# A four-layer modulated convolution on one core: a shorter first chain, a third pair of output banks, and row ends blurred on VectorE

## The chip, the cores and the metric

The kernel runs on one core of a Trainium2 chip. The metric is the device time of one execution in microseconds. Each execution is one launch over all 128 samples. TensorE (PE in the profile, its weight loads PEld) does the matrix products, VectorE (DVE) and ScalarE (ACT) read its results from PSUM and do the vector work, GpSimd (POOL) does small vector work in SBUF, and SyncE (SP) issues nearly all transfers.

## The reference, cut to what matters

Every sample has its own weights: a style vector of 128 numbers is mapped to one scale per input channel and layer, and the scaled weights are normalised for every output channel. Four convolution layers of 64 channels follow, and the input is added to their result.

```python
def _layer(x, style, w, b, mw, mb, typ):
    s = style @ mw.T + mb
    weight = SCALE * w * s[:, None, :, None]
    demod = lax.rsqrt(jnp.sum(weight * weight, axis=(2, 3)) + EPS)
    weight = weight * demod[:, :, None, None]
    if typ == 'same':
        out = vmap(_conv_same)(x, weight) + b
    elif typ == 'upsample':                 # stride 2, then blur
        out = _blur(vmap(_conv_up)(x, weight) + b, 2.0 * blur_k, (1, 1))
    elif typ == 'downsample':               # blur, then stride 2
        out = vmap(_conv_down)(_blur(x, blur_k, (2, 2)), weight) + b
    return out
...
for i, typ in enumerate(('same', 'upsample', 'same', 'downsample')):
    out = _layer(out, style, weights[i], biases[i], mod_w[i], mod_b[i], typ)
return x + out          # x: 128 x 64 x 1024, float32
```

The blur kernel is (1, 3, 3, 1)/8. No nonlinearity stands between the layers, so all four collapse, for each sample, into one convolution with nine taps. Only the first and last three columns of a row differ, because of the padding.

## The kernel before

**The work.** Two samples make a pair `p` (64 pairs), four samples, or two pairs, a step `q` (32 steps, `p = 2q` and `2q + 1`). For each `q` the combined weights are made by a chain of matrix products: `scale3` scales the last layer's weights (`wd`), `stage1` multiplies them with layer 2 (`psS`, copied to `S`), `stage2` with the blurred layer 1 (`psR`, copied to `R`), `stage3` in two parts with layer 0 (`psW`, copied to `Wf`). `combine` makes sums `H` of them for a fast convolution. On the data side `pre1` and `pre2` make sums `T` (and `G` on the way) of the input planes `X`: two operations on VectorE for `G`, two for `T` (lines 478 and 479, by default on GpSimd), and `pre2a` and `pre2b` on VectorE. `convA12` and `convA3` multiply three of these sums with `H` into a PSUM tile `psA`. `seed1` combines these into `u`, `v` and `y1`, and `seed2` writes two sums into the output banks `Y`. `convB` adds two further products to what lies in `Y`. `output` scales, adds the constant and moves the result to `o`, and `store` sends it off. So VectorE must have written `Y` (`seed2`) before TensorE may start `convB` of that pair, and it may write `Y` only after the outputs of the pair before have been read.

**The banks.** PSUM has two buffers of two banks for `ps_conv` (in turn `psM`, some `psS`, `psR`, all `psA`), two banks for `ps_w` and two for `Y`. From the last steps on, `Y2` turns the pair of `ps_w` into a second pair of output banks, for pairs 60 and 62; pairs 61 and 63 stay on `Y`. `zeros_to_y` runs products of zeros over a pair of output banks before its first use. Two early calls of it (lines 845 and 851) stand where TensorE would otherwise have nothing to do.

**The order.** The order of each engine's instructions is that of the program; it is written out by hand. Lines 839 to 919 are the prologue. The first 16 samples (`PART[0]`) come first: `mod_matmul` and `mod_scale` give the layers' scales, `var_matmul` (line 204), `var_root` and the Newton steps give the norms. Layer 2's norm is inverted first (`first_inverse`), since `table_A` and with it `scale3(0)` need it; those of the other layers follow (`var_inverse`, `var_newton`, lines 866 and 867). `blur_matmul` (line 288) needs the transfer `par_oi`. Two later groups of samples (`PART[1]`, `PART[2]`) get their scales and norms later; `mod_matmul(LATER)` in line 871 makes the scales of both.

**The main loop**, lines 993 to 1077, has the same order for each `q`: `stage2(q+2)`, `convB(p)`, its outputs, `stage3(q+2, 0)`, `convA12(p+2)`, VectorE work for later pairs, `stage3(q+2, 1)`, `convA3(p+2)`, `convB(p+1)`, its outputs, VectorE work, `stage1(q+3)`, `scale3(q+4)`, `combine(q+2)`, `convA12` and `convA3` of `p+3`. The first steps and the last two differ a little.

**The row ends.** The first and last three columns of all rows are computed apart and layer by layer, in `SLOTS` (small groups of matmuls between the two products of a `convB`) and `EXTRA` (VectorE work at the two halves of a step). For the last layer `setup2` blurs its weights into six taps `g3`, and `ends3` runs those six taps over `Ve`, the end columns of layer 2's output.

## Time and profile before

| | |
|---|---|
| time, median of 3 runs | 503.1 us (502.73 to 504.3) |
| time of the profiled execution | 505.0 us |
| its span, first to last instruction | 503.2 us |
| mean granted TensorE clock | 0.995 |
| TensorE busy | 490.7 us, 98% of the span |
| VectorE busy | 438.9 us, 87% |
| ScalarE busy | 322.3 us, 64% |
| GpSimd busy | 127.7 us, 25% |
| DMA | 70.90 MB, mean 141 GB/s |

A record in the profile has a start, a duration and the engine's idle time before it, with what ended that idle time. Matmuls are pipelined [...], so the duration of one (304 ns) says less than the distance between two starts; every matmul of the program leaves two records. In the timeline, neighbouring records of one kind are merged: a row gives the first start, the time to the last end and how many there are.

### The profile page before, as it was taken

The page shows a single profiled execution, that of the slowest core. Times are in us where ns is not written, and L with a number is a line of the kernel's source. Part 1 is how long each engine was busy: PE and PEld are TensorE (multiplying, and loading weights), DVE is VectorE, ACT ScalarE, POOL GpSimd, SP SyncE. Part 2 cuts the span into 40 slices and gives each one's busy share as a digit, 9 for nine tenths or more (in the row PEclk, how much of TensorE's full clock was granted, in tenths as well). Part 3 has the DMA queues.
Part 4 walks back from the last instruction along what each step waited for, and adds up shares of the span by engine and source line. Part 5 has one row for each costly group of instructions (what it writes and reads, how often), then busy time and mean ns, then how long its engine had stood idle before and what let it go on. Part 6 is the DMA issues. An engine that isn't in the chain of part 4 may idle for free.

```text
span 503.2 us, 28357 instructions
## 1 busy us (share of the span) xinstructions
PE 490.7 (98%) x12644; PEld 479.4 (95%) x12644; DVE 438.9 (87%) x932; ACT 322.3 (64%) x785; POOL 127.7 (25%) x192
## 2 busy tenths in 40 slices
PE   8999899999999999999999999999999999999994
PEld 5889799999999999999999999999999999999994
DVE  4789989999999979988979999879988879888895
ACT  3446466676676666676677666657667657667653
POOL 3414122334222122122222122212212212222210
PEclk9999999999999999999999999999999999999999
DMA  8115544444444444443544444435454435443123
GB/s 258 59 45 171 179 128 131 160 145 142 142 157 149 151 142 138 148 147 122 157 144 148 132 154 153 146 128 162 125 164 146 139 120 185 138 151 129 66 107 126
DMA packets 37161, 70.90 MB, mean 141 GB/s; under 512 B 4144, under 2 KB 28464, under 8 KB 37040
## 3 DMA queue, kind: packets, MB, share of 16 engines
q1 hardware_dynamic: 36960, 68.85, 42.3%
q8 instruction: 99, 1.62, 1.4%
q10 hardware_dynamic: 80, 0.25, 0.1%
q14 instruction: 22, 0.18, 0.1%
HBM read 35.46 MB, written 33.62 MB: 137 GB/s over the span
## 4 chain that ended last, share of the span: by engine, by line
PE 85%; DVE 10%; ACT 2%; issue 1%; DMA 1%; DVEq 0%
PE psA L516 28%; PE Y L516 20%; PE psR L365 15%; PE psW L402 13%; PE psS L334 6%; PE psE L747 2%; DVE Y L549 2%; DVE T L498 1%; PE Y L170 1%; DVE G L469 1%; ACT o L595 1%; DVE T L488 1%; PE psM L189 1%; DVE v L549 1%; DVE G L472 1%
## 5 line engine op out<-in xcount | busy, mean ns | idle before, releaser
L516 PE MATMUL psA<-T,H 64*64 64x170 f32 x4608 | 207.7, 304 | 0.9 <-DVE H L443 0.9
L516 PEld LDWEIGHTS psA<-T,H 64*64 64x64 f32 x4608 | 191.2, 133 | 1.5 <-ACT R L312 1.2
L516 PE MATMUL Y<-T,Wf 64*64 64x170 f32 x3072 | 143.2, 307 | 4.3 <-DVE Y L549 4.3
L478 POOL TENSOR_TENSOR T<-G 128x342 f32<-128x342 f32 x60 | 55.1, 919 | 338.2 <-DVE G L472 193.5
L516 PEld LDWEIGHTS Y<-T,Wf 64*64 64x64 f32 x3072 | 130.5, 134 | 5.7 <-issue 3.9
L595 ACT ACTIVATE o<-Y,oc,dm 128x340 f32<-128x340 f32 (+1 forms) x126 | 80.0, 635 | 58.8 <-PE Y L516 56.5
L549 DVE SCALAR_TENSOR_TENSOR Y<-psA,u 128x340 f32<-128x340 f32 (+1 forms) x132 | 66.4, 507 | 42.4 <-ACT o L595 40.2
L402 PE MATMUL psW<-R,par_oi 64*64 64x256 f32 (+3 forms) x1536 | 100.4, 349 | 0.0
L365 PE MATMUL psR<-S,E 64*64 64x192 f32 (+1 forms) x2304 | 94.0, 299 | 0.0
L312 ACT ACTIVATE Wf<-psW,t 128x256 f32<-128x256 f32 (+1 forms) x252 | 75.5, 382 | 22.9 <-PE psW L402 22.9
L402 PEld LDWEIGHTS psW<-R,par_oi 64*64 64x64 f32 x1536 | 87.0, 133 | 2.3
L365 PEld LDWEIGHTS psR<-S,E 64*64 64x64 f32 x2304 | 86.5, 133 | 0.8 <-ACT Wf L312 0.3
L312 ACT ACTIVATE R<-psR,tC 128x448 f32<-128x448 f32 x63 | 36.6, 631 | 56.7 <-PE psR L365 56.7
L595 ACT ACTIVATE o<-y,oc,dm 128x170 f32<-128x170 f32 x125 | 65.7, 526 | 0.0
L498 DVE TENSOR_TENSOR T<-G 128x684 f32<-128x684 f32 x64 | 56.1, 877 | 0.0
L469 DVE SCALAR_TENSOR_TENSOR G<-X 128x688 f32<-128x688 f32 x64 | 55.4, 866 | 0.0
L479 POOL TENSOR_TENSOR T<-G 128x342 f32<-128x342 f32 x60 | 55.3, 922 | 0.0
L334 PE MATMUL psS<-wd,par_oi 64*64 64x192 f32 x768 | 46.2, 332 | 0.1
L334 PEld LDWEIGHTS psS<-wd,par_oi 64*64 64x64 f32 x768 | 38.0, 137 | 1.3 <-ACT wd L312 0.3
L543 ACT ACTIVATE m<-psA 128x340 f32<-128x340 f32 x64 | 29.3, 457 | 11.6 <-PE psA L516 6.5
L549 DVE SCALAR_TENSOR_TENSOR y<-psA,v 128x340 f32<-128x340 f32 x64 | 32.7, 511 | 2.2
L549 DVE SCALAR_TENSOR_TENSOR u<-psA,m 128x340 f32<-128x340 f32 x64 | 32.2, 503 | 0.5 <-ACT m L543 0.5
(127 smaller groups left out, 386.2 us busy)
## 6 DMA issues: line engine op xcount, KB each, us to landing
out<-o SPq DMA_DIRECT2D x128, 255.0 KB, 2.8
X<-in_x SPq DMA_DIRECT2D x60, 344.0 KB, 3.1
X<-in_x SPq DMA_DIRECT2D x60, 172.0 KB, 3.0
X<-in_x SPq DMA_DIRECT2D x4, 516.0 KB, 6.9
Xe<-in_x_ends SPq DMA_DIRECT2D x1, 512.0 KB, 3.7
par_oi<-in_params_oi SPq DMA_DIRECT2D x2, 208.0 KB, 4.8
par_io<-in_params_io ACTq DMA_DIRECT2D x1, 240.0 KB, 3.8
par_io<-in_params_io SPq DMA_DIRECT2D x1, 240.0 KB, 4.4
```

The lines of the kernel that those rows point to most:

```text
L312: nc_a.activation(dst, src, AF.Copy, scale=f)
L334: nc.tensor.matmul(ps[r][cols, k * C : (k + K) * C], woi[rows, 2, k, :], src[rows, :], start=(k == 0), stop=(k == K - 1), skip_group_check ...
L365: nc.tensor.matmul(ps[r][cols, lo * C : (lo + m) * C], E[rows, e // 2 + 1 + (e % 2) * 5, :], src[rows, a, :], start=(n == 0), stop=(n == 8 ...
L402: nc.tensor.matmul(ps[r][cols, (lo - t_lo) * C : (hi - t_lo) * C], woi[rows, 0, k, :], rt[c][rows, lo - k : hi - k, :], start=(k == order[0]),
L469: nc_v.scalar_tensor_tensor(g[:, PL:], X[:, : 2 * PL], 0.5, X[:, PL:], op0=ALU.mult, op1=ALU.subtract)
L478: eng.tensor_add(t[:, 2, :NJ], plane(g, 2), plane(g, 1))
L479: eng.tensor_sub(t[:, 3, :NJ], plane(g, 2), plane(g, 1))
L498: nc_v.tensor_sub(t[:, 0:2, :NJ], both(a, PL), both(b, 1))
L516: nc.tensor.matmul(ps[s][cols], w, Ts[p][rows, SLOT[m], j : j + NB], start=(g == 0 and m not in (0, 4)), stop=(g == 2), skip_group_check=True,
L543: nc_a.activation(m1, m[0], AF.Copy, scale=-1.0)
L549: nc_v.scalar_tensor_tensor(out, x, f, y, op0=ALU.mult, op1=ALU.add)
L595: nc_a.activation(dst, src, AF.Identity, bias=add, scale=d3)
```

## The change

**Prologue.** Layer 2 goes alone through square, sum, `var_matmul`, `var_root` and `first_inverse`. The squares of layers 0 and 1 (VectorE) and 3 (ScalarE), their sums and their `var_matmul` come later, the latter between the matmuls of `stage1(0)` and the copies of its result. Half of the second group of zero products is left out. `mod_matmul(LATER)` moves from before `stage2(0)` to after `stage2(1)`, into a buffer of its own (`psL`), and what hangs on it (`mod_scale(PART[1])`, tables) moves too. The constant products of layers 1 and 2 for `PART[0]` and `var_matmul(PART[1])` come later, the last into free columns of an output bank. The sums of the first input pairs are reordered: `pre1(0)` is split into its two operations for `G` and the two for `T`, with copies of the weight chain between them. The norms of `PART[1]` (`var_inverse`, `var_newton`, `table_A`, tables) move from the prologue into the first step. In that step `pre1(4)` and `pre1(5)` lose the argument `nc_v`, so that lines 478 and 479 run on GpSimd for them, `seed1(3)` comes ahead of `pre1(5)`, and in step 1 `seed2(3)` comes ahead of `pre1(6)`.

**Last pair.** Pair 63 gets a third pair of output banks, taken from `ps_conv`, with its own `zeros_to_y`; its whole `seed` then runs in step 30. Its stores are split into columns of the first third and of the other two thirds.

**Row ends.** `g3` and `setup2` go. `blur_side` adds neighbouring columns of `Ve` three times (six operations on VectorE, steps 20 to 23), which is the blur (1, 3, 3, 1) without its factor; `ends3` then has three taps with the plain weights, and `rest3` multiplies by 0.125.

```diff
-        nc_v.tensor_mul(ssq[:, :, bs], sc[:, :, bs], sc[:, :, bs])
...
+    def mod_square(bs, ls=slice(0, NL)):
+        nc_v.tensor_mul(ssq[:, ls, bs], sc[:, ls, bs], sc[:, ls, bs])
+
+    def q2_sum(ls):
+        nc_v.tensor_add(q2[T, ls], wsq[T, ls, 0, :], wsq[T, ls, 1, :])
+        nc_v.tensor_add(q2[T, ls], q2[T, ls], wsq[T, ls, 2, :])
...
-            return rest
+            return g01, g2, rest
...
-    def store(p, s):
-        nc.sync.dma_start(out[p, :, s], os[p][:, s])
+    def store(p, s, at=slice(0, 3 * NB)):
+        nc.sync.dma_start(out[p, :, s, at], os[p][:, s, at])
...
+    def blur_side(s, part):
+        at = (2 * s, 0, 0)[part]
+        src = (Ve[s], Ue[s], Ve[s])[part][:, :, at : at + 10 - part]
+        dst = (Ue[s], Ve[s], Ue[s])[part][:, :, : 9 - part]
+        nc_v.tensor_tensor(dst, src[:, :, :-1], src[:, :, 1:], op=ALU.add)
+
     def ends3(ps):
...
-            6,
-            lambda i, r, c: g3[:, i, :],
-            lambda i, r, c: Ve[c][:, :, i + 2 * c : i + 2 * c + 5 : 2],
+            K,
+            lambda i, r, c: wio[:, 3, i, :],
+            lambda i, r, c: Ue[c][:, :, i : i + 5 : 2],
...
-    nc_a.activation(wsq[T, :2], wio[T, :2], AF.Square)
-    nc_v.tensor_mul(wsq[T, 2:], wio[T, 2:], wio[T, 2:])
+    nc_a.activation(wsq[T, L2], wio[T, L2], AF.Square)
     blur_scale()
-    zeros_to_y(4, 256)
+    zeros_to_y(2, 256)
     mod_scale(PART[0], pm[0][0])
-    nc_v.tensor_add(q2[T], wsq[T, :, 0, :], wsq[T, :, 1, :])
-    nc_v.tensor_add(q2[T], q2[T], wsq[T, :, 2, :])
-    for table_of in (table_B, table_0, table_02):
-        table_of(PART[0])
-    var_matmul(PART[0], pm[0][1])
-    var_root(PART[0], pm[0][1])
+    mod_square(PART[0])
+    q2_sum(L2)
+    table_B(PART[0])
+    weight_sums()
+    var_matmul(PART[0], pm[0][1], (2,))
+    nc_v.tensor_mul(wsq[T, L01], wio[T, L01], wio[T, L01])
+    var_root(PART[0], pm[0][1], L2)
+    nc_a.activation(wsq[T, L3], wio[T, L3], AF.Square)
     psB = [Y[:, r] for r in range(2)]
     blur_matmul(psB)
-    weight_sums()
     first_inverse(PART[0])
     table_A(PART[0], d2)
     scale3(0, BOTH)
+    q2_sum(L01)
     blur_copy(psB, BOTH)
+    q2_sum(L3)
+    table_0(PART[0])
+    table_02(PART[0])
+
+    def rest_of_var():
+        var_matmul(PART[0], pm[0][1], (0, 1, 3))
+
+    stage1(0, None, BOTH, rest_of_var)
+    var_root(PART[0], pm[0][1])
+    scale3(1)
+    scale3(2)
     var_inverse(PART[0])
     var_newton(PART[0])
...
-    stage1(0, None, BOTH)
-    mod_matmul(LATER, pm[1][0])
-    scale3(1)
-    nc_a.copy(raw[0][:, 0, :n_later], pm[1][0][:, :n_later])
-    scale3(2)
-    pre1(0, nc_v)
...
+    g01, g2, t12 = pre1(0, None)
+    g01()
+    stage2(0, None, BOTH)
+    zeros_to_y(2, 512)
+    const_first(0, PART[0])
+    g2()
+    t12(nc_v)
+    pre2a(0)
+    stage3(0, 0, None, BOTH)
+    stage1(1, ps_conv)
+    pre2b(0)
+    g01, g2, t12 = pre1(1, None)
+    g01()
+    stage3(0, 1, None, BOTH)
+    stage1(2, ps_conv)
+    combine(0)
+    const_rest(0, PART[0], const_of(0, PART[0]))
+    stage2(1, ps_conv)
+    psL = unit(ps_conv, "psL")
+    mod_matmul(LATER, psL[0])
+    nc_a.copy(raw[0][:, 0, :n_later], psL[0][:, :n_later])
+    convA12(0)
+    convA3(0)
...
     stage3(1, 1)
+    const_first(2, PART[0])
+    var_matmul(PART[1], var_of(PART[1]), start=False)
     convA3(1)
+    pre1(2)
+    pre2(2)
+    const_rest(2, PART[0], const_of(2, PART[0]))
+    var_root(PART[1], var_of(PART[1]))
     combine(1)
-    pre2a(2)
+    seed1(1)
     pre1(3)
-    seed1(1)
-    pre2b(2)
-    var_inverse(PART[1])
-    var_newton(PART[1])
-    table_A(PART[1], dm[:, 2, PART[1]])
-    for of in (table_C, vector_c0, table_3, vector_Da):
-        of(PART[1])
...
-        (17, 0): lambda: setup2(0),
-        (17, 1): lambda: setup2(1),
...
+        (20, 1): lambda: blur_side(0, 0),
+        (21, 0): lambda: blur_side(1, 0),
+        (21, 1): lambda: blur_side(0, 1),
+        (22, 0): lambda: blur_side(1, 1),
+        (22, 1): lambda: blur_side(0, 2),
+        (23, 0): lambda: blur_side(1, 2),
...
-        if q == NQ - 1:
-            seed2(p + 1)
...
-            for i in range(2):
-                store(p + 1, i)
+                    if i != 2:
+                        store(p + 1, r, slice(0, NB) if i == 0 else slice(NB, HO))
...
+            if q == 1:
+                seed2(p + 1)
             pre1(p + 4)
             store(p, 1)
-            seed(p + 1)
+            if q > 1:
+                seed(p + 1)
...
             seed2(p + 1)
             pre2(p + 3)
-            pre1(p + 4, nc_v)
+            var_inverse(PART[1])
+            var_newton(PART[1])
+            table_A(PART[1], dm[:, 2, PART[1]])
+            for of in (table_C, vector_c0, table_3, vector_Da):
+                of(PART[1])
+            pre1(p + 4)
...
             seed(p + 2)
-            seed1(p + 3)
+
+            Y2[p + 3] = unit(ps_conv, "Y3")
+            zeros_to_y(2, 2 * NB, p + 3)
+            seed(p + 3)
...
             pre2(p + 4)
-            pre1(p + 5, nc_v)
...
+        if q == 0:
+            seed1(p + 3)
+            pre1(p + 5)
```

## The prediction

> **What bounds the kernel now.** I read the page's first part, then the waits of TensorE, then the timeline around each of these waits, then the granted clock there.
>
> ```profile
> PE 490.7 (98%) x12644; PEld 479.4 (95%) x12644; DVE 438.9 (87%) x932; ACT 322.3 (64%) x785; POOL 127.7 (25%) x192
> ...
> PE Y L516 <- DVE Y L549: 4.3, 4, 2.3
> ...
> 44.13 1.10 PE L516 MATMUL Y<-T,Wf 64*64 64x170 f32 x24 [0.71 <-DVE Y L549]
> ...
> 59.82 1.06 DVE L549 SCALAR_TENSOR_TENSOR Y<-psA,u 128x340 f32<-128x340 f32 x2
> ...
> 61.03 1.70 PE L516 MATMUL Y<-T,Wf 64*64 64x170 f32 x24 [2.26 <-DVE Y L549]
> ...
> 495.57 1.96 PE L516 MATMUL Y<-T,Wf 64*64 64x170 f32 x48 [1.04 <-DVE Y L549]
> ```
>
> TensorE is the bound. In the timeline the `stage2` groups (L365) of steps without a slot start exactly 14.39 us apart (365.87, 380.26, 394.66), and between 66 and 480 us its waits sum to 0.3 us. So only three things can pay: matmuls left out, idle stretches of TensorE in the prologue and the first two steps, and the tail. VectorE needs 12.4 us of a plain step, so it has 2 us to spare later; but from 40 to 60 us it is busy 9.65 and 9.90 of each 10, which is why `convB(1)` and `convB(3)` wait for `seed2`.
>
> ```profile
> 6.80:10.20 3.40, 3.28 (x72) 3.05 (x74) 1.78 (x8) 1.05 (x3) 2.30 (x8) 1.00 1.00 397
> 10.20:13.60 3.40, 3.40 (x40) 2.46 (x36) 2.84 (x8) 1.35 (x4) 1.34 (x4) 1.00 0.46 178
> 58.00:61.40 3.40, 1.14 (x35) 0.85 (x31) 3.33 (x9) 1.41 (x5) 1.78 (x2) 1.00 0.96 356
> 61.40:64.80 3.40, 3.40 (x57) 3.40 (x52) 3.24 (x6) 0.28 (x2) 0.06 (x1) 0.50 0.44 140
> ```
>
> The columns are the stretch, its length and busy time of PE, PEld, DVE, ACT, POOL, then clock and DMA. After a stretch in which TensorE was busy 1.14 of 3.40 us, the next 3.4 us ran at clock 0.50: 57 records where the stretch after it has 98. So the wait of 2.26 us cost about 1.7 us more. From `stage2` at 49.45 to the next at 68.09 step 1 took 18.64 us, 4.25 above 14.39.
>
> **The change part by part.** All sums are against the profiled execution (span 503.2, 505.0 us with what lies around it). I apply the difference to the median, 503.1.
>
> *1. Up to the first stages.*
>
> ```profile
> 7.24 2.59 PE L288 MATMUL Y<-w1s,par_oi 64*64 64x128 f32 x56
> 9.95 2.20 PE L334 MATMUL psS<-wd,par_oi 64*64 64x192 f32 x24
> 12.08 1.70 PE L189 MATMUL psM<-par_s 128*64 128x112 f32 x16
> 13.71 2.73 PE L365 MATMUL psR<-S,E 64*64 64x192 f32 x72
> ...
> 26.06 2.83 PE L516 MATMUL psA<-T,H 64*64 64x170 f32 x72 [0.89 <-DVE H L443]
> ```
>
> Layer 2 alone lets `var_root` start when ScalarE has finished its four `w1s` (6.69) instead of 7.46; the chain root to `wd` (7.46 to 9.45) then brings `wd` at about 8.7. But `stage1(0)` also stands behind `blur_matmul`, which needs `par_oi`: issued at 1.78 and 2.37, 4.7 to 4.9 us to landing, so 7.2. It starts as now, `stage1(0)` too: **the 0.8 us won on the chain are worth 0**. `mod_matmul(LATER)` (1.63 us in the chain of waits) then leaves the place before `stage2(0)`. In its place stand 12 records of `var_matmul` (16 take 0.87, from 6.37 to 7.24, so 0.65), and `S` is ready at 12.9: `stage2(0)` starts at 13.0, 0.7 earlier.
>
> From there by starts in the timeline (`stage1` 1.0, `stage2` 2.55, `stage3` 1.3 and 0.97, zeros 0.85, a `convA` pair 2.6): zeros 15.5, `stage3(0,0)` 16.5, since `R` waits on VectorE behind `g01` until 16.4; `stage1(1)` 17.8; `stage3(0,1)` 18.8, when VectorE has copied `Wf` behind `g2`, the two `T` sums and `pre2a`; `stage1(2)` 19.8; `stage2(1)` 20.8; `mod_matmul(LATER)` 23.35, now 0.85 instead of 1.70, as 53 ns a record at twice the early rate; `convA12(0)` 24.75, when ScalarE has emptied `psR`. `H` is ready at 22.8, no longer last. That is 1.3 before 26.06, but 24 small records (0.85) are still to come, so **`stage2(2)` starts at 33.1 instead of 33.6: -0.5**.
>
> [...] `stage1(0)` has 92 ns a record, 55 at 19.13. Half the zeros and the filler before `stage2(0)` go. [...] 3.28 busy of 3.40 did not do, 3.40 of 3.40 did, since `stage2` at 13.71 is fast. By the row alone `stage2(0)` is fast at 13.0 too: 0. [...] I take **+1.0**[...].
>
> *2. The first two steps.* VectorE's chain by starts: `combine` 2.86, `pre1` without lines 478/479 1.21, `pre2` 1.21, `seed` 2.35 (`seed2` 0.97), the norms of `PART[1]` 1.71 (41.20 to 42.91). With TensorE 0.5 earlier, `seed2(1)` can start when ScalarE has read pair 0's outputs, at 40.9 (41.38 now), and ends at 41.9; TensorE wants `convB(1)` at 42.2. The wait of 0.7 to 0.85 goes: **-0.8**. Then `pre2(3)` 43.1, norms 44.8, `pre1(4)` 46.0, `seed(2)` 48.3, `combine(2)` 51.2, `pre2(4)` 52.4, `seed1(3)` 53.8, `pre1(5)` 55.0, `pre2(5)` 56.2, `seed2(3)` 57.3. TensorE reaches `convB(3)` 14.39 + 9.1 after 33.1, at 56.6: a wait of about 0.75 stays, of 2.4 (start to start) before, and too short to halve the clock (0.85 us of gap at 43.1 did not): **-1.65 and -1.7**. The two `pre1` cost VectorE 0.85 less each; GpSimd takes 1.85 each and is 25% busy. Late next is `seed(5)`: 15.1 us of VectorE work (with 1.5 of `mod_scale`, its square and a constant, as at 70.14) against 14.5 of TensorE: **+0.5**. After it VectorE gains over 1 us a step. Sum -3.65; bounds, by an error of 1 us in this chain: -2.2 and -4.9. ScalarE's queue and the loads (3 us to landing, needed a step later) are not late.
>
> *3. The row ends.*
>
> ```profile
> L747 PE MATMUL psE<-Ve,g x48: 388/394/404, 404.6 to 407.5; 64*64 64x192 f32 x48
> L793 DVE SCALAR_TENSOR_TENSOR Ue<-b1s,Ue x2: 747/748/748, 270.8 to 285.2; 128x576 f32<-128x576 f32 x2
> ```
>
> The step with `ends3` is 411.82 - 394.66 = 17.16, so 48 records cost 2.77 us; 24 go: **-1.4**. VectorE loses four operations of 0.35 and gets six over 9 columns of 64 samples, 576 elements or, once, fewer: 0.75 each by the row above, 4.5 in all. Cover: 12.4 of 14.39 us a step, at most two of them in a step, 13.9; in step 20 one with `rest2(1)`, 14.7 for once, out of a lag that the next step makes up. 0, at worst +0.5.
>
> *4. The tail.* `convB(63)` waits 1.04 (1.2 by starts) for `seed2(63)`, which stood behind the outputs of pair 61. In its own banks it is done while `convB(62)` runs. New are 8 records of zeros, 0.6 us as at 480.2; they wait for `seed(62)`, done at 491.65, before TensorE is free at 492.9. So -0.5. The four last reads of the shared pair of banks still alternate between ScalarE and VectorE, as from 497.59 to 499.59: both tiles are one pair, and VectorE keeps its wait. The last transfer is two thirds of the size; from 499.59 to 503.2 it takes 3.6, others there 2.3 to 2.6: -0.3, bounds 0 and -1. **-0.8**.
>
> Sum: -0.5 + 1.0 - 0.8 - 1.65 - 1.7 + 0.5 - 1.4 - 0.8 = -5.35, so **497.7 us** (profiled execution 499.6).
>
> **The rivals.**
> - *Slower, by the clock.* [...] Work of 9 us more runs at half rate, in place of the +1.0: 505.7. It decides against the change from about 8 us of loss on, a clock granted after 29 us. For it: 3.28 busy of 3.40 was not enough. Against it: at half rate `stage2(0)` alone is 5 us without a gap. 4%.
> - *The wait at `convB(3)` stays long.* If VectorE's chain is 1 us later than I have it, TensorE waits 1.75 there, and the clock falls again: +1.0 + 1.7, 500.4. For it: VectorE has hardly an idle microsecond from 41 to 73. 18%.
> - *The filler was worth its time.* [...] +2.4 against the forecast, 500.1. 15%.
> - *Nothing waits.* Clock granted as now, chain 0.8 earlier, no lag at `seed(5)`: -1.0 - 0.75 - 0.5, 495.4. 13%.
> - *Only the matmuls left out and the tail count*, and VectorE's work in the first steps is merely moved so that the waits come back elsewhere: 503.1 - 2.2 + 1.0 = 501.9. For it: the norms of `PART[1]` stay in the same stretch. Against it: 1.7 us of lines 478/479 leave VectorE, and `seed2(3)` passes `pre1(6)`. 5%.
> - The forecast has the other 45%, with a range of its own of 496.5 to 499.
>
> **The numbers.** A measurement of this kernel tells 0.3%, 1.5 us, from no change: faster is below 501.6, slower above 504.6. The range of 495.0 to 500.6 leaves out the slower and the fifth case and the edges of the others. Faster 0.91, the same 0.05, slower 0.04.
>
> **What would show it.** `stage1(0)` near 9.9, `stage2(0)` near 13.0 and its 72 records in 2.7 us (right) or over 4 (clock late); first `psA` group near 24.8; the wait at `convB(1)` gone; under 1.3 us of wait before `convB(3)` and no stretch of clock 0.50 after it; 24 records of `psE<-Ue,par_io` with 192 elements; no wait before the last `convB`, whose outputs still alternate. I am wrong if TensorE waits for VectorE by 2 us or more anywhere before 75 us, or if the steps from 20 to 24 are longer than 14.39.

## The result, and the profile after

Over 8 runs the changed kernel takes 501.53 us (median; 500.11 to 502.28), the kernel before on the same chip 504.33 (8 runs, 502.73 to 505.19): a ratio of 0.9947, with a 95% interval of 0.9929 to 0.9965. It is faster, by about 0.5%, half of what was forecast; 497.7 and the whole range of 495.0 to 500.6 are too low. The profiled execution spans 499.8 us, 3.4 less than the one before, where 5.35 were forecast.

The profile after, in the order in which that of before was read. The first part of the page, and the first row of TensorE's waits:

```profile
PE 487.3 (97%) x12620; PEld 476.7 (95%) x12620; DVE 443.5 (89%) x937; ACT 323.0 (65%) x787; POOL 135.2 (27%) x195
...
PE Y L534 <- DVE Y L567: 3.1, 3, 1.5
```

TensorE is busy 3.4 us less; 1.4 of it are matmuls left out, and 1.65 a half-clock stretch that is missing, of which more below. VectorE has 4.6 us *more*, although the change takes `T` sums from it. And TensorE's waits for the seeds in `Y` (now L534 on L567) have gone from 4.3 us in four to 3.1 in three only. Here they are, in TensorE's timeline (start, length, engine, line, operation, count; in brackets the idle time before it and what ended it), behind two rows of the prologue:

```profile
12.62 3.06 PE L377 MATMUL psR<-S,E 64*64 64x192 f32 x72
...
25.03 2.25 PE L534 MATMUL psA<-T,H 64*64 64x170 f32 x56 [0.33 <-ACT R L324]
...
58.82 1.10 PE L534 MATMUL Y<-T,Wf 64*64 64x170 f32 x24 [1.47 <-DVE Y L567]
...
75.23 1.05 PE L534 MATMUL Y<-T,Wf 64*64 64x170 f32 x21 [1.34 <-DVE Y L567]
```

`stage2(0)` starts at 12.6 instead of 13.7 and the first `psA` group at 25.0 instead of 26.1. The wait at `convB(1)` is gone, that at `convB(3)` has fallen from 2.26 to 1.47, and one of 1.34 is new, at `convB(5)`. The forecast had 0.75 and 0.5 there. Now the granted clock around `convB(3)`, in stretches (columns as before):

```profile
57.60:61.00 3.40, 2.18 (x61) 2.21 (x65) 3.37 (x8) 0.56 (x4) 3.40 (x15) 1.00 0.87 285
61.00:64.40 3.40, 3.40 (x93) 3.27 (x88) 3.40 (x5) 3.40 (x8) 2.88 (x3) 1.00 0.96 331
```

No stretch runs at 0.50. VectorE is busy for 3.37 and 3.40 us of the two, and GpSimd (fifth column) for all of the first. The two engines' timelines show what VectorE is busy with. First VectorE:

```profile
32.91 1.58 DVE L516 TENSOR_TENSOR T<-G 128x684 f32<-128x684 f32 x1
...
56.10 1.59 DVE L516 TENSOR_TENSOR T<-G 128x684 f32<-128x684 f32 x1
57.62 1.06 DVE L567 SCALAR_TENSOR_TENSOR Y<-psA,u 128x340 f32<-128x340 f32 x2
...
60.22 0.87 DVE L516 TENSOR_TENSOR T<-G 128x684 f32<-128x684 f32 x1
61.00 1.59 DVE L483 SCALAR_TENSOR_TENSOR G<-X 128x688 f32<-128x688 f32 x1
62.51 1.22 DVE L488 SCALAR_TENSOR_TENSOR G<-X 128x342 f32<-128x342 f32 x1
```

then GpSimd:

```profile
47.34 0.91 POOL L494 TENSOR_TENSOR T<-G 128x342 f32<-128x342 f32 x1
...
55.90 1.06 POOL L494 TENSOR_TENSOR T<-G 128x342 f32<-128x342 f32 x1 [6.77 <-DVE G L488]
56.93 1.56 POOL L495 TENSOR_TENSOR T<-G 128x342 f32<-128x342 f32 x1
...
60.31 1.55 POOL L494 TENSOR_TENSOR T<-G 128x342 f32<-128x342 f32 x1
61.81 1.54 POOL L495 TENSOR_TENSOR T<-G 128x342 f32<-128x342 f32 x1
```

The same instruction of `pre2b` (L516) takes 0.87 at 60.22 and 1.58 or 1.59 at 32.91 and 56.10; one of `pre1` (L483) takes 1.59. Each long row began while one of GpSimd's two `T` sums (L494, L495) was running, and the sums are long as well, up to 1.56 instead of 0.91. The ends of the rows show how: here the two engines took turns. The sum at 55.90 ends at 56.96 and the L516 beside it at 57.69, 0.73 later; the next sum ends 0.80 after that. The L516 at 60.22 began *before* the sum at 60.31 and keeps its 0.87; that sum ends 0.77 after it, and L483 ends 0.73 after that sum. So in these rows the one that began second ended 0.73 to 0.80 us after the first: of the 0.87 and 0.91 us that the two take alone, most lies behind the other's end. At 47.34, where VectorE forms a seed from PSUM, the sum keeps its 0.91. Measured against the median of their own kind (operation, tiles and shape) in the same profile, VectorE's instructions of the first 120 us lasted 0.7 us too long in all before the change, and 4.0 after it. This sum is called VectorE's surplus below.

The rest of the change: the row for `ends3` in the list of its tile's instructions, and the last output in VectorE's timeline.

```profile
L763 PE MATMUL psE<-Ue,par_io x48: 388/496/613, 327.7 to 404.2; 64*64 64x512 f32 x24, 64*64 64x192 f32 x24
```

```profile
495.18 0.45 DVE L615 TENSOR_SCALAR o<-Y,dm,oc 128x170 f32<-128x170 f32 x1 [0.56 <-ACT o L613]
```

The 24 records with 192 elements are the new `ends3`; step 24 is 15.79 us instead of 17.16, the steps 20 to 23 keep their 14.39. The last output ends 29.6 us after the last `stage2` instead of 30.2.

### The profile page after: what moved, and what is told of

Its sections match the earlier page's. It is cut to its first block, busy times and chain, and to the rows that moved or that the text cites. A ratio compares the mean times of both kernels' runs of the same rounds, so it can differ in the third digit from the quotient of the medians.

```text
span 499.8 us, 28326 instructions
## 1 busy us (share of the span) xinstructions
PE 487.3 (97%) x12620; PEld 476.7 (95%) x12620; DVE 443.5 (89%) x937; ACT 323.0 (65%) x787; POOL 135.2 (27%) x195
## 3 DMA queue, kind: packets, MB, share of 16 engines
q8 instruction: 99, 1.62, 1.4%
## 4 chain that ended last, share of the span: by engine, by line
PE 84%; DVE 11%; DMA 2%; issue 1%; ACT 1%; SPq 0%; DVEq 0%; ACTq 0%
PE psA L534 28%; PE Y L534 20%; PE psR L377 15%; PE psW L414 12%; PE psS L346 6%; PE psE L763 2%; DVE Y L567 2%; DVE T L516 1%; DVE G L483 1%; DMA par_oi<-in_params_oi 1%; DVE u L567 1%; DVE v L567 1%; DVE G L488 1%; DMA out<-o 1%; DVE T L506 1%
## 5 line engine op out<-in xcount | busy, mean ns | idle before, releaser
L534 PE MATMUL psA<-T,H 64*64 64x170 f32 x4608 | 208.8, 304 | 0.3 <-ACT R L324 0.3
L534 PEld LDWEIGHTS psA<-T,H 64*64 64x64 f32 x4608 | 191.8, 133 | 1.2 <-ACT R L324 0.5
L534 PE MATMUL Y<-T,Wf 64*64 64x170 f32 x3072 | 141.9, 304 | 3.1 <-DVE Y L567 3.1
L494 POOL TENSOR_TENSOR T<-G 128x342 f32<-128x342 f32 x62 | 58.0, 935 | 315.7 <-DVE G L488 187.3
L534 PEld LDWEIGHTS Y<-T,Wf 64*64 64x64 f32 x3072 | 129.5, 133 | 4.7 <-ACT m L561 3.4
L567 DVE SCALAR_TENSOR_TENSOR Y<-psA,u 128x340 f32<-128x340 f32 (+1 forms) x134 | 66.7, 502 | 36.8 <-ACT o L613 34.1
L495 POOL TENSOR_TENSOR T<-G 128x342 f32<-128x342 f32 x62 | 59.4, 957 | 0.0
L516 DVE TENSOR_TENSOR T<-G 128x684 f32<-128x684 f32 x64 | 57.8, 903 | 0.0
L483 DVE SCALAR_TENSOR_TENSOR G<-X 128x688 f32<-128x688 f32 x64 | 56.3, 879 | 0.0
L567 DVE SCALAR_TENSOR_TENSOR y<-psA,v 128x340 f32<-128x340 f32 x64 | 32.7, 511 | 2.2
L488 DVE SCALAR_TENSOR_TENSOR G<-X 128x342 f32<-128x342 f32 x64 | 33.4, 521 | 0.0
```

The costliest lines, as they stand in the source:

```text
L483: nc_v.scalar_tensor_tensor(g[:, PL:], X[:, : 2 * PL], 0.5, X[:, PL:], op0=ALU.mult, op1=ALU.subtract)
L488: nc_v.scalar_tensor_tensor(plane(g, 2), plane(X, 3), 0.5, plane(X, 2), op0=ALU.mult, op1=ALU.subtract)
L494: eng.tensor_add(t[:, 2, :NJ], plane(g, 2), plane(g, 1))
L495: eng.tensor_sub(t[:, 3, :NJ], plane(g, 2), plane(g, 1))
L516: nc_v.tensor_sub(t[:, 0:2, :NJ], both(a, PL), both(b, 1))
L534: nc.tensor.matmul(ps[s][cols], w, Ts[p][rows, SLOT[m], j : j + NB], start=(g == 0 and m not in (0, 4)), stop=(g == 2), skip_group_check=True,
```

## The experiments

The steps are numbered from the first `stage2` of the loop, `stage2(2)`: step 0 lies between `stage2(2)` and `stage2(3)`. A step without a side job is 14.39 us, so the waits of this kernel can be read from the starts of `stage2` alone. All times of steps below are start to start, from each kernel's profile. The runs are from three chips, on which the kernel before (its executions of mean clock 0.997 or more) takes 503.02 to 503.05 us, so the times of different rows can be compared; the ratio is to the executions of the kernel before beside each run.

```
                steps 0 to 6 (us)                            sum     median, ratio to before (95%)
before          15.86 18.64 15.20 14.52 14.40 15.01 14.57   108.2   
before, again   15.87 16.99 15.18 14.52 14.40 15.01 14.57   106.5   503.44 (one run)
after           14.58 16.56 16.96 14.52 14.40 15.01 14.56   106.6   501.53  0.9947 (0.9929-0.9965)
e_after         14.86 16.46 16.79 14.52 14.40 15.01 14.56   106.6   501.18  0.9948 (0.9932-0.9965)
e_memset        14.43 16.34 15.17 14.52 14.39 15.04 14.56   104.5   499.07  0.9906 (0.9884-0.9928)
e_memset_xe     14.43 15.16 15.63 14.52 14.39 15.00 14.57   103.7   498.43  0.9883 (0.9861-0.9906)
e_order         14.43 14.48 15.78 16.21 14.67 15.08 14.57   105.2   499.66  0.9919 (0.9896-0.9942)
e_order2        14.44 14.48 15.32 16.29 14.68 15.09 14.57   104.9   499.81  0.9916 (0.9892-0.9941)
e_order2_xe     14.44 14.48 15.32 16.29 14.67 15.10 14.57   104.9   499.47  0.9910 (0.9888-0.9932)
e_order3_xe     14.44 14.48 15.33 14.52 15.47 16.79 17.00   108.0   503.16  0.9996 (0.9979-1.0012)
e_sum5_dve      14.43 18.52 15.41 14.52 14.40 15.01 14.56   106.9   501.00  0.9961 (0.9949-0.9974)
e_store_whole   14.44 17.20 16.47 14.52 14.39 15.01 14.57   106.6   501.35  0.9949 (0.9928-0.9970)
e_no_y3         14.44 16.69 17.01 14.51 14.40 15.03 14.57   106.7   501.50  0.9969 (0.9956-0.9981)
e_ends_only     15.86 18.66 15.19 14.52 14.40 15.03 14.57   108.2   502.69  0.9991 (0.9978-1.0003)
```

Three lines of it hold the main finding: the first seven steps of the changed kernel are no shorter (106.6) than those of the kernel before in its second profile (106.5), and with GpSimd's reads taken away they are 2.1 us shorter.

**e_after: the changed kernel again.** No edit.

> The changed kernel once more, on the chip of the runs beside it. Theory A (VectorE and GpSimd hold each other up: an addition or subtraction of VectorE with both inputs in SBUF that runs while GpSimd forms its two T sums takes about 1.6 us instead of 0.86, and the T sum about 1.5 instead of 0.92) and rival B (VectorE simply has too much queued before seed2(3) and seed(5); the long rows are an accident of that one profile): 501.5 us. A: the same instructions are long again, at 32.9, 42.2, 56.1, 61.0 and 62.5 us, and the waits before convB(3) and convB(5) are 1.5 and 1.3 us. B: the long rows sit elsewhere or are gone, and the two waits stay all the same.

501.18 us, ratio 0.9948. The long rows are at the same five instructions (L516 with 1.58 to 1.59 at 32.2, 41.5 and 55.4 us, L483 with 1.59 at 60.3, L488 with 1.23 at 61.8) and the waits have the same size (gaps of 1.72 and 1.62 from start to start before `convB(3)` and `convB(5)`, 1.77 and 1.65 in the first profile). They belong to the kernel, not to one execution. As A had it.

**e_memset: the sums of five pairs replaced by writes.**

```diff
         def rest(eng):
+            if p in (2, 3, 5, 6, 7):
+                eng.memset(t[:, 2, :NJ], 0.0)
+                eng.memset(t[:, 3, :NJ], 0.0)
+                return
             eng.tensor_add(t[:, 2, :NJ], plane(g, 2), plane(g, 1))
```

> For pairs 2, 3, 5, 6 and 7 GpSimd fills the two T planes with zeros (two memsets, which read nothing) instead of forming the two sums; their outputs lack these sums. VectorE's instructions and their order are the same. Theory A: the four pre2b and G rows that took 1.58 fall to 0.86, and the one of 1.22 to 0.51; VectorE is 2.2 us earlier at seed2(3) and 3.6 at seed(5), the waits of 1.5 and 1.3 us before convB(3) and convB(5) go, and the time falls by 2.8 us (2.2 to 3.0), to 498.7. Rival B: the waits and the time stay within 0.4 us.

499.07 us, 2.1 less than e_after beside it. VectorE's program is untouched, and the long rows of its timeline are gone, at all three places of `pre2b`:

```profile
33.16 0.87 DVE L520 TENSOR_TENSOR T<-G 128x684 f32<-128x684 f32 x1
...
42.44 0.86 DVE L520 TENSOR_TENSOR T<-G 128x684 f32<-128x684 f32 x1
...
55.63 0.86 DVE L520 TENSOR_TENSOR T<-G 128x684 f32<-128x684 f32 x1
```

VectorE's surplus in the first 120 us falls from 4.0 to 0.3 us. `seed2(3)` starts 22.96 us after `stage2(2)` instead of 24.42; the two waits for VectorE are gone. So theory A holds and B is out: VectorE has time for this order, if GpSimd doesn't read beside it. But step 1 was still 16.34 long. TensorE's timeline says what came in place of the waits:

```profile
57.62 1.10 PE L538 MATMUL Y<-T,Wf 64*64 64x170 f32 x24 [0.45 <-ACT Wf L324]
...
63.58 0.94 PE L538 MATMUL psA<-T,H 64*64 64x170 f32 x19 [0.94 <-issue]
```

Before `convB(3)` TensorE waits 0.45 us for ScalarE's copy of `Wf`. Then, inside `convA3(5)`, it stands from 62.34 to 63.58 (start to start) for "issue": nothing that the profile shows. The next kernel asks what that is.

**e_memset_xe: one load moved out of the burst.**

```diff
         if q == 1:
-            nc.sync.dma_start(Xe, x_ends)
             zeros()
+        if q == 4:
+            nc.sync.dma_start(Xe, x_ends)
```

> e_memset with one more edit: the load of the row ends' inputs (Xe, 512 KB) is issued in step 4 instead of step 1. In e_memset no wait for VectorE was left in step 1, yet it still took 16.34 us from stage2 to stage2: TensorE stood for 1.24 us inside convA3(5), with no releaser in the profile, 1.4 us after a block of its instructions (16 KB) had come 9.3 us after the one before it, in a stretch in which the DMA engines were full. Theory F (the next block of instructions waits behind data transfers): with Xe gone from the burst the block comes sooner after the one before it (7 us or less), the gap goes, step 1 takes 14.5 to 15.2, and the time falls by 1.0 (0.5 to 1.4) from e_memset's, to 498.1. Rival G (that gap has a cause inside TensorE or its data): it stays at 1.2 us, same time.

The gap is gone and step 1 is 15.16, 1.18 shorter, as F had it; step 2 gives 0.46 back, and the time falls by 0.6 us to 498.43, at the low end of what was expected. What F rests on are blocks of 16 KB of a DMA queue that the profile calls "instruction". It brings 99 of them, and TensorE has 25,240 records, so 255 to a block if all of them are TensorE's; at the 196 records that ran in 3.40 us (e_before, below) that is an estimated 4.4 us of TensorE's work. The starts of the blocks, read from the trace:

```
e_memset       43.6  48.4  51.9  61.2  65.2  69.0     TensorE stands 62.34 to 63.58
e_memset_xe    42.8  46.2  50.9  58.4  63.7  68.2     no gap
e_order        43.9  47.5  52.5  58.1  64.7  68.5     TensorE stands 66.29 to 66.94
e_store_whole  44.3  48.2  52.0  61.3  65.7  70.2     TensorE stands 63.08 to 63.73
after          44.5  49.5  53.3  61.2  64.8  68.8     no gap (waits for VectorE 57.05 to 58.82)
```

Mostly one comes every 4 to 5 us and takes 0.9 to 2. In three of the profiles one starts 6.6 to 9.3 us after the one before it, TensorE stands, and goes on 1.3 to 1.6 us after that block's end (61.2 + 0.96, then 63.58; 64.7 + 0.94, then 66.94; 61.3 + 0.90, then 63.73). The distance alone does not decide: in e_memset_xe a block comes 7.5 us after the one before it, more than the 7 that F allowed, and nothing stands. The DMA engines are nearly full before and during the late block (in e_memset share 0.95 from 57.8 to 61.2 and 1.01 from 61.0 to 64.4, both 335 GB/s). That the block is late *because* of the data rests on one edit, with one profile on each side; that TensorE was out of instructions is inferred from the times.

**e_order: the same instructions in another order on VectorE.**

```diff
+    pre1(2)
     seed(0)
...
-    pre1(2)
     pre2(2)
...
             seed2(p + 1)
-            pre2(p + 3)
             var_inverse(PART[1])
...
+            pre2(p + 3)
             pre1(p + 4)
...
+            if q == 1:
+                seed2(p + 1)
+            if q == 2:
+                seed(p + 1)
             if q < NQ - 2:
                 pre2(p + 3)
             store(p, 0)
-            if q == 1:
-                seed2(p + 1)
             pre1(p + 4)
             store(p, 1)
-            if q > 1:
+            if q > 2:
                 seed(p + 1)
...
+        if q == 1:
+            seed1(p + 2)
         if q:
             pre2(p + 4)
...
-        if q < NQ - 2:
+        if q == 1:
+            seed2(p + 2)
+        elif q < NQ - 2:
             seed(p + 2)
...
-            seed1(p + 3)
             pre1(p + 5)
+            seed1(p + 3)
```

> Every instruction of the changed kernel, on the same engines, but VectorE's order in the first steps is such that after each pre1 (which starts GpSimd's two T sums) come instructions that read PSUM (a seed) or the norms, not pre2 or the next pre1. Theory A: the long rows go, no wait before convB(3) and convB(5), -2.8 us (2.0 to 3.0), 498.7; against the kernel before about -5.6, which is what was forecast for the change without its clock term. Rival B: the order alone takes pre2(5) from ahead of seed2(3) and pre2(7) and pre1(8) from ahead of seed(5), so the waits fall too, but the rows keep their 1.6 us and some wait of 0.5 or more appears before convB(4) or later; -1 to -2 us.

499.66 us, 1.5 less than e_after: in B's interval, not in A's. The steps 0 and 1 are as short as they can be (14.43, 14.48), but VectorE's surplus is still 3.8 us, only elsewhere: `pre2b` of pair 8 and L483 of pair 9 take 1.58 each at 74.5 and 76.0, `pre2a` of pair 2 1.24 at 31.8, `residual` (L444) 0.93 instead of 0.28 at 64.7. Step 3 then pays 1.35 us (start to start) at `convB(7)`. So this run gained by doing first what TensorE wants first, and not by keeping the two engines apart, which its order failed to do: the sums of a pair last 1.84 us, a `seed1` 1.45, and what follows it reads SBUF twice again.

**e_order2 and e_order2_xe: step 2 mended as well.** e_order with

```diff
-        if q == 1:
+        if q in (1, 2):
             seed1(p + 2)
...
-        if q == 1:
+        if q in (1, 2):
             seed2(p + 2)
         elif q < NQ - 2:
```

and the second with the load of `Xe` moved as in e_memset_xe.

> e_order with VectorE's order also mended in step 2: seed1(6) stands between pre1(8) and pre2(8), as in step 1, so that GpSimd's sums of pair 8 run beside reads of PSUM. In e_order the collision had moved there (pre2b(8) and G of pair 9 took 1.58 each at 74.5 and 76.0 us) and TensorE waited 1.1 us before convB(7). Theory A: those rows fall to 0.86, the wait before convB(7) goes, -1.1 (-0.6 to -1.5) from e_order, 498.6. Rival B (the lag is VectorE's load, not the collisions): the wait appears one step later, same time as e_order within 0.3.

> e_order2 with the load of Xe in step 4 instead of step 1. Theories A and F together: no wait for VectorE and no late block of instructions in the first four steps, each 14.4 to 15.0 us from stage2 to stage2; about -0.5 from e_order2 (its gap in e_order, 66.3 to 66.9, was 0.65), 498.1, against the kernel before -5.4, the size of the forecast. Rival: the block is late elsewhere, since each step moves the same bytes; no gain over e_order2.

499.81 and 499.47 us, hardly different from e_order's 499.66. The rows of 1.58 are gone, but in the steps 2 and 3 three others are long (1.02 at L506, 0.93 and 0.95 at L444), the surplus is 3.5 us, and the gap before `convB(7)` grew to 1.86. My -1.1 was a miss. The -0.5 for the move of `Xe` came as -0.3, which is within the scatter of these runs (499.23 to 500.61 and 499.31 to 500.24), and there was no late block left to mend: that of e_order is not there in either, not even in e_order2, which loads `Xe` when e_order does. So a block can be on time without that move, too.

**e_order3_xe: the order kept up to step 5.** e_order2_xe with `2 <= q < 6` for the seed ahead of `pre2` in a step's first half and `1 <= q < 6` for `seed1` in its second.

> e_order2_xe with its order (the seed ahead of pre2 in the first half of a step, seed1 between pre1 and pre2 in the second) kept up to step 5. In e_order2_xe steps 0 and 1 were near 14.4, but VectorE, still behind, made TensorE wait 1.6 us before convB(7) in step 3, where the order fell back. If VectorE's lag is only carried along until its slack of 2 us a step takes it up, seed(7) 2.4 us earlier ends that wait: -1.5 (-1.0 to -1.8) from e_order2_xe, 497.9. Rival: the lag shows at convB(9) or convB(8) instead; same time.

503.16 us: all is lost again. `convB(7)` no longer waits (step 3 is 14.52), and the steps 4 to 6 take 15.47, 16.79 and 17.00. In TensorE's timeline the next large wait is

```profile
111.66 1.96 PE L534 MATMUL Y<-T,Wf 64*64 64x170 f32 x48 [1.96 <-DVE Y L567]
```

`convB(10)`, in step 5, the last one with that order. The rival had the waits moving on, and so they did, but it had the time unchanged, and 3.7 us were lost. My idea of a lag that VectorE's slack takes up was wrong. The order brings a collision of about 0.65 us or more to every step from 2 to 6 (VectorE's surplus is 5.0 us up to 120 us), and the slack of 2 us a step isn't there yet: in after, VectorE is idle for only 0.35, 0.39 and 0.76 us of the steps 4, 5 and 6. The extra collisions (1.5 us more surplus than in e_order2_xe) are less than the 3.7 us that were lost; the rest stays open.

**e_sum5_dve: the sums of one pair back on VectorE.**

```diff
             seed1(p + 3)
-            pre1(p + 5)
+            pre1(p + 5, nc_v)
```

> The changed kernel with the two T sums of pair 5 on VectorE again (two of 0.5 us, 0.42 to 0.43 from start to start, 0.85 in all). Theory A: GpSimd no longer runs beside pre2b(5), whose 1.58 falls to 0.86, so moving the sums to GpSimd had won 0.85 and lost 0.72: seed2(3) and the wait before convB(3) (1.5) move by +0.1, the time by less than 0.3. As the forecast counted it (sums on GpSimd cost VectorE nothing): seed2(3) 0.85 later, the wait 2.3, +0.85 us, 502.0.

501.00 us, -0.2 against e_after. VectorE's timeline there:

```profile
56.95 0.86 DVE L516 TENSOR_TENSOR T<-G 128x684 f32<-128x684 f32 x1
57.73 1.07 DVE L567 SCALAR_TENSOR_TENSOR Y<-psA,u 128x340 f32<-128x340 f32 x2
```

`pre2b(5)` is back at 0.86, and `seed2(3)` starts 24.67 us after `stage2(2)` (57.73 - 33.06) where it was 24.42: 0.25 later, not 0.85. Having moved pair 5's sums to GpSimd was worth a quarter of a microsecond at `seed2(3)`. The wait there rose more, from 1.47 to 2.09, since TensorE came 0.35 us sooner in this profile, and it was followed by a half-clock stretch; with that, step 1 was 18.52. The whole doesn't show it (its four other executions, of mean clock 0.996 or more, took 500.45 to 501.88, and this one 501.36). Step 2 became 1.5 shorter, as only 0.3 us of wait were left before `convB(5)`.

**e_before: the kernel before, profiled again.** No edit.

> The kernel before, profiled once more: how much of its waits and of its prologue is the same in a second execution. If the half-clock stretch after the wait before convB(3) (61.4 to 64.8 us in the first profile, worth 1.7 us in the forecast) belongs to the kernel, it is there again; [...] it may be missing, and the wait of 2.3 us remains. The start of stage2(2), 33.6 in the first profile, is expected within 0.5.

Span 501.7 instead of 503.2, `stage2(2)` at 33.33. The waits are the same four (4.3 us, longest 2.3), and the half-clock stretch isn't there. In stretches:

```profile
57.80:61.20 3.40, 1.13 (x32) 0.85 (x28) 3.33 (x9) 1.35 (x5) 1.77 (x2) 1.00 1.00 358
61.20:64.60 3.40, 3.40 (x100) 3.40 (x96) 3.26 (x7) 1.85 (x5) 1.42 (x2) 1.00 0.40 123
```

The same gap of 2.57 us, nearly the same work in 3.40 us (1.13, then 1.14), and full clock after it: 100 records where the first profile has 57. Step 1 is 16.99 instead of 18.64; the stretch cost 1.65 us, as it was priced, but it isn't in every execution. The section on why the prediction was wrong says in which it can be expected.

**e_store_whole: the last pair stored whole.**

```diff
                     output(p + 1, r, eng, ((i, i + 1),))
-                    if i != 2:
-                        store(p + 1, r, slice(0, NB) if i == 0 else slice(NB, HO))
+            for r in range(2):
+                store(p + 1, r)
```

> The last pair's two outputs are stored whole (255 KB each, after the last output) instead of in thirds and two thirds. Theory T1 (four small transfers in flight together end later than they are issued earlier: the last two of 170 KB took 3.3 us from issue to landing, while the whole ones before took 2.6): the last lands 2.6 us after its issue, -0.4 us (-0.2 to -0.7), 501.1. Rival T2 (a transfer's landing at the end depends on what else is under way, not on its size): no difference, within 0.2 us; or later by 0.3 because a whole store is the larger one.

501.35 against 501.18: T2, no difference. The last bytes do move sooner when the stores are split: 1.6 to 1.7 us after the last output in the ten profiles with split stores, 1.9 in the four with whole ones. But from the last output to the end of the span it is 4.1 us here and 3.6 to 4.2 in the others, whole or split, so those 0.3 us are lost in that scatter, and so are the 0.6 us that the first profile of after had over that of before.

**e_no_y3: no third pair of banks.** `seed2(p + 1)` stands again ahead of `output(p, 1)` in the last step, and step 30 has

```diff
-            Y2[p + 3] = unit(ps_conv, "Y3")
-            zeros_to_y(2, 2 * NB, p + 3)
-            seed(p + 3)
+            seed1(p + 3)
```

> The changed kernel without the third pair of banks: seed2(63) goes into Y again, behind pair 61's reads, as before the change. If the third pair is worth what the trace of after shows, the last output ends 30.2 us after the last stage2 instead of 29.6, and the time is 0.6 longer than e_after's (501.8). Rival: what comes after the last output (3.6 to 4.2 us in the six profiles so far, whatever the stores) hides it, 0 to 0.2.

The last `convB` waits 1.04 us for VectorE again and the last output ends 30.21 us after the last `stage2`, 0.60 later. The time is 0.3 longer than e_after's, and the intervals of the two ratios overlap: the trace shows the 0.6 us, the time of the whole can't tell 0 from 0.6.

**e_ends_only: the row ends alone, on the kernel before.** `blur_side` and its six calls, `ends3` over `Ue` with `wio[:, 3]`, `rest3` with 0.125, and no `setup2`.

> The kernel before with one part of the change alone: the row ends' last inputs blurred on VectorE (six sums), their weights no longer, so 24 matmuls of ends3 instead of 48. Theory E (what the change won is the row ends, 1.4 us, the rest of its gain in the first steps being given back to collisions): -1.4 us against the kernel before, step 24 15.8 instead of 17.2, steps 20 to 23 unchanged at 14.4; this is over half of the whole change's 2.7. Rival: the six sums cost TensorE something in steps 20 to 23, and the gain is under 0.7.

In its profile step 24 is 15.79 instead of 17.16, the steps 20 to 23 are 14.39 or 14.40: -1.37 us, as in after. The time shows 0.4 (-1.1 to +0.2), less than that. Its profile (mean clock 0.993) has a half-clock stretch after the wait before `convB(3)` (step 1 is 18.66). Its five executions of 0.993 have a median of 503.68 us, 1.6 under the kernel before's 505.28 in its executions of low clock; the nine others have 502.42, only 0.6 under its 503.05 (both figures are explained in the next section). So the step shows 1.4 us; the time of the whole neither confirms nor refutes it.

## Why the prediction was wrong

**The mechanism that failed is in part 2, "The first two steps".** Its sentence "The two `pre1` cost VectorE 0.85 less each; GpSimd takes 1.85 each and is 25% busy" counted work on another engine as free. It wasn't free here: a `T` sum that reads SBUF on GpSimd and an instruction with both inputs in SBUF on VectorE did not run together. The one that began second was held up, by about 0.72 us in most of these rows. e_memset agrees: with writes in place of GpSimd's reads, 1.58 became 0.86. And the ends of the rows (0.73 to 0.80 us apart, above) put most of the second one's time behind the first one's end. Both engines' rows got longer (0.86 to 1.58 and 0.91 to 1.56) because two sums and two such instructions follow each other and each in turn was second. In the kernel before, `pre1` was mostly followed by a seed, which reads PSUM, and the two lived side by side (0.50 and 0.92 us, in the rows below). The change puts `pre2` or another `pre1` behind it. Both cases stand in the first profile of before, in VectorE's timeline and in GpSimd's, and could have been read there:

```profile
38.59 0.50 DVE L549 SCALAR_TENSOR_TENSOR u<-psA,m 128x340 f32<-128x340 f32 x1
39.01 0.50 DVE L549 SCALAR_TENSOR_TENSOR v<-psA,m 128x340 f32<-128x340 f32 x1
39.54 0.51 DVE L549 SCALAR_TENSOR_TENSOR y<-psA,v 128x340 f32<-128x340 f32 x1
39.97 1.30 DVE L498 TENSOR_TENSOR T<-G 128x684 f32<-128x684 f32 x1
...
38.75 0.92 POOL L478 TENSOR_TENSOR T<-G 128x342 f32<-128x342 f32 x1 [7.92 <-DVE G L472]
39.63 0.91 POOL L479 TENSOR_TENSOR T<-G 128x342 f32<-128x342 f32 x1
```

The seed's three rows keep 0.50 beside the sums; `pre2b` (L498) takes 1.30 and ends 0.73 after the second sum.

**Part 2, by its terms.** Forecast -0.8 - 1.65 - 1.7 + 0.5 = -3.65. The wait at `convB(1)` went, as said. `seed2(3)` was put 23.2 us after `stage2(2)` (56.3 - 33.1); it came at 24.42 with the collisions and would have come at 22.96 without (e_memset). So the wait at `convB(3)` fell by 0.8 instead of 1.65, and the lag at `seed(5)`, put at +0.5, came to 1.8 in step 2 (16.96 instead of 15.18), two more long rows being on its way. Measured: -1.60 against the first profile, +0.06 against the second. With GpSimd's reads gone (e_memset) the seven steps sum to 104.5, 3.7 less than in the first profile of before, the size of the forecast; this is partly luck, since a late block and a wait for `Wf` stand in step 1 there, which the forecast did not have. Neither of the two signs that I had named for being wrong came up: no single wait reached 2 us. They looked for one large wait, and two of 1.5 and 1.3 were enough.

**The term of 1.7 for the half clock** was right for the profiled execution and wrong for the median. That could have been read from the numbers at hand: the profiled execution took 505.0 us, more than any of the three timed runs (502.7 to 504.3). Of 59 executions of the kernel before with a granted clock on record, 38 have a mean of 0.997 to 0.999 and a median of 503.05 us; 21 have 0.994 to 0.996 and 505.28. The profile came from the second group. In the text the difference made against it was applied to a median of 503.1, which belongs to the first, where those 1.7 us had never been spent. (That the stretch is what parts the two groups is shown by one profile of each.) Against the second profile the sum would have been -3.65 instead of -5.35, and 499.45. For the same reason the 2.8 us between the two medians of the result are mixed: against 503.05, the changed kernel's 501.53 is 1.5 us less.

**The clock term of the prologue (+1.0)**, an estimate of mine that no row of the trace showed (nor the later clocks of the rivals at 505.7 and 500.1), was not paid. After the change the full clock was on record from 13.1 us on, from 13.6 before, and in the other profiles of both from 9.5 to 13.6, with `stage2(0)` taking 2.9 to 3.3 us for 72 records instead of 2.7. This error of about 0.9 has the other sign and hid part of the one above. The rest of part 1 looks right in the first profile of after: `stage1(0)` 9.8 (about 9.9), `stage2(0)` 12.6 (13.0), first `psA` group 25.0 (24.8), `stage2(2)` 33.2, -0.4 (-0.5). But the other profiles don't bear out a gain. With the prologue of before, `stage2(2)` starts at 33.59, 33.33 and 32.42 (e_ends_only); with the changed one, in eleven profiles, at 32.40 to 33.55. It goes with the moment of the full clock: full from 13.6 on, it starts at 33.59 before and 33.55 after the change (e_order), from 12.0 to 12.2 on at 33.33 and 33.45 (e_memset), from 9.5 and 10.4 on at 32.42 and 32.40 (e_memset_xe). So that the shorter first chain won anything is not shown.

**The row ends (-1.4)** measured -1.37, in all twelve profiles with the new `ends3`, and the six sums on VectorE cost nothing: the steps 20 to 23 keep 14.39.

**The tail (-0.8)**: -0.6 for the outputs (-0.5), confirmed by e_no_y3; the -0.3 for the smaller last transfer came for the bytes (1.9 to 1.6 us) and did not reach the end of the span (e_store_whole). Outputs still alternate between ScalarE and VectorE, as forecast.

Put together from the second profile of before (span 501.66) to after (499.85): -0.13 up to `stage2(2)`, +0.06 in the steps 0 to 2, -1.38 up to the last `stage2`, -0.36 behind it, -1.8 in all. That is the fifth rival, "only the matmuls left out and the tail count", to which I gave 5% and 501.9 us. Its picture was right: VectorE's waits came back elsewhere. That its number is so near is partly luck, for its sum holds the +1.0 for the clock, which wasn't paid. What I held against it, the two sums taken from VectorE, was the very thing that failed.

What could be had with the same work: the e_order kernels, 499.5 to 499.8 us, beat both; e_memset_xe at 498.4, which leaves out the sums of five pairs, shows about what there would be to gain if the two engines didn't meet in the first steps. Open is an order that keeps GpSimd's sums beside PSUM reads in every early step; three orders tried here didn't find it.

## What to carry to other kernels

When work moves to GpSimd, look at what VectorE runs in the same microseconds: beside an instruction of VectorE with two SBUF inputs next to nothing was gained (0.72 us lost for 0.85 won), beside one that reads PSUM it was free (a seed's rows stayed at 0.50 us), and an order that is right for TensorE can pair them wrongly. Before a difference is made against a profiled execution, ask whether that execution is a typical one: its own time against the runs, and every half-clock stretch in it is to be taken as a chance, not as a cost (one of the two profiles of the kernel before had it). And where three waits stand in a row, removing the first uncovers the next: here VectorE (1.47 us before `convB(3)` in after), then ScalarE's copy (0.45 in e_memset), then a standstill (1.24 there) that goes with a late block of instructions.

## What the runs showed of the hardware

The granted clock after the same wait was not the same in each profile. In the first profile of before, the stretch at 0.50 after it is on record with 3.413 us, and the stretches of full clock last whole multiples of that: 47.79 us is 14 of them and 436.91 is 128 there, 484.69 is 142 in after. The full clock begins at another moment in each profile, 9.5 to 13.6 us after the first instruction. It is at 13.59 us in the first profile of before and at 12.18 in the second; counted on from there in lengths of 3.413 us, one length is 57.96 to 61.37 in the first and two are 56.55 to 59.96 and 59.96 to 63.37 in the second. The gap before `convB(3)` (58.47 to 61.03, and 58.21 to 60.78) lies in one length in the first, which was followed by 3.41 us at half clock, and is cut in two in the second, which was not. The other three: whole in one length at 2.39 us (e_sum5_dve) and at all but 0.03 of 2.58 us (e_ends_only), half clock; whole in one length at 2.07 us (e_store_whole), none. Here are that length and the next, first for e_store_whole, then for e_sum5_dve (columns as before):

```profile
55.54:58.95 3.41, 1.64 (x47) 1.36 (x41) 3.38 (x6) 1.49 (x5) 3.41 (x11) 1.00 0.70 180
58.95:62.36 3.41, 3.41 (x102) 3.41 (x98) 3.41 (x6) 2.03 (x5) 3.41 (x8) 1.00 1.01 338
...
55.97:59.38 3.41, 1.32 (x38) 1.04 (x32) 3.38 (x7) 1.48 (x5) 0.00 (x0) 1.00 0.77 219
59.38:62.79 3.41, 3.41 (x58) 3.41 (x54) 3.41 (x5) 0.45 (x2) 2.54 (x2) 0.50 0.91 271
```

So of the gaps that lay in one length (or all but 0.03 us of them), those of 2.39 us and more (start to start) were followed by half clock, and that of 2.07 was not; these are four profiles, and the counting in lengths is mine. The same wait is 1.72 to 2.09 us in the four profiles of kernels with the changed first steps as they are (after, e_after, e_store_whole, e_no_y3), under 2.39 us, but not by much: the mean clock was 0.996 to 0.998 in the 21 executions of the changed kernel, and 0.993 in one of the 14 of the other two.

In three profiles TensorE stood for 0.65, 0.65 and 1.24 us with no releaser on record, each time behind a late 16 KB block of the "instruction" queue. That it had run out of instructions, and that full DMA engines made the block late, was not shown.
